# Two dense blocks handed to the gather, W2 in single steps, casts on ScalarE: one relational graph layer

## The chip, the cores and the metric

The kernel runs on one core of a Trainium2 chip. A core has TensorE (PE, matrix products; its weight loads, PEld, run beside them), VectorE (DVE), ScalarE (ACT), GpSimd (POOL) and SyncE (SP, which here only issues transfers). Sixteen DMA engines serve all queues. The metric is the device time of one execution in microseconds (us); the kernel before is given by the median of three runs, and one execution was profiled.

## The reference: what is computed

A graph of 3125 nodes with 128 features and 100000 edges, sorted by destination, each with one of 8 types, goes through four layers. The first three (three GCN steps, one sum over in-edges with a linear map, one GIN layer with batch norm) are not touched. The fourth is a relational layer applied twice, with 128 to 256 and 256 to 128 features:

```python
def rgcn_layer(x, src, dst, etype, W, W_root, b, num_rels):
    h = jnp.einsum('ni,rio->rno', x, W)
    msg = h[etype, src]
    seg = dst * num_rels + etype
    sums = jax.ops.segment_sum(msg, seg, num_segments=N * num_rels)
    cnt = jax.ops.segment_sum(jnp.ones(msg.shape[0], x.dtype), seg, num_segments=N * num_rels)
    mean = sums / jnp.maximum(cnt, 1.0)[:, None]
    agg = mean.reshape(N, num_rels, do).sum(axis=1)
    return agg + x @ W_root + b

h = jax.nn.relu(rgcn_layer(x, src, dst, edge_type, W1, root1, b1, 8))
h = rgcn_layer(h, src, dst, edge_type, W2, root2, b2, 8)
x = _layernorm(x + h)
```

For each node and each edge type it takes the mean over the in-edges of that type, maps it with that type's weights and adds the eight. The kernel must return the last x, 3125 x 128 in fp32.

## The kernel before

The nodes are cut into 25 blocks of 128 (the last one partly filled). Tile, the layer above the instruction set, puts in the semaphores and decides the order of each engine's instructions when the program is built: it goes by the order in which the program was written, and moves a later instruction ahead where by its own times an earlier one is not ready. On the chip each engine then follows its fixed order.

**Lists and masks.** `relations()`, a generator that is advanced while the GCN steps run, prepares what the relational layers need. It counts in-edges by type, gathers the edge lists of the blocks that will be "gathered" (`NG` of them, 34 lists of 128 edges a block, 15 for the last; lines 373 to 423), and then builds, for the `ND` = 14 "dense" blocks, a count matrix per type: how many edges run from node s to node d, as bytes in DRAM (`rel`, lines 425 to 466). Edges of the other 11 blocks stay as lists: `gsrc` holds the source row, `gkey` the place of destination and type within a window of 24 nodes. If a list doesn't fit its window, a flag makes the whole fallback `general` run.

**First relational layer, preparation (lines 831 to 838).** `split2` splits x into two fp32r parts, `xs`. `store3` splits it again into three bf16 parts and writes them to DRAM as the row table `xt_d` (7 chunks; a ScalarE copy, a DVE subtract, a ScalarE copy, a DVE subtract, a store on SP's queue; two buffers). No gather can start before the whole table is written.

**Dense blocks (lines 881 to 887, `relation` at 752).** The blocks go in chunks of four or three (`CH`; the first four chunks are the 14 dense blocks). For each chunk and each of 8 types, five groups: a byte mask is loaded, cast to fp32r (two of five groups on ScalarE, line 766, three on DVE, line 768, by the tuple `casts`), and multiplied by the two parts of x, ten products a group (line 771). Masks have six byte buffers and three cast ones. 4 x 8 x 5 = 160 groups; the product of a type is scaled into `z`.

**Gathered blocks (`gathered`, line 782), between the groups.** It is a generator: a step is one tile, in which POOL gathers 128 table rows (an indirect DMA into one of twelve `gx` buffers, line 805) and TensorE multiplies the three bf16 parts by a one-hot matrix that DVE made (lines 797 and 813), or the end of a block, `put1`. After each dense group, `relation` advances it by `rate` = 2.2 steps on average, beginning 14 steps late; what is left is done after the last dense group.

**A finished chunk (`linear1`, line 840).** When the eight types of a chunk are summed, dense or gathered, W1 and the root map are applied (16 fp32 products and two more, lines 851 and 853), then ReLU into `hT`; then, for each block, twice: two fp32 products with W2 for four types (line 861) and `store3` into the DRAM table `ht_d`. The profile records an fp32 product as two.

**Second relational layer.** It is built the same way on `ht_d`, type by type, with all casts on ScalarE (line 944), the same `CH`, the same 14 dense blocks and the rate 2.2. Its first gather waits for all of `ht_d`.

Of the kernel before, what the change touches and what calls it, by code (L numbers as in the profile page):

```python
# [21 lines left out]
P = 128  # L22
# [36 lines left out]
HL = 49 * 64  # L59
ND = 14  # L60
NG = NB - ND
GT = [34] * (NG - 1) + [15]
# [10 lines left out]
def listed(ctx: ExitStack, tc: tile.TileContext, p: dict, out: bass.AP, bad):  # L73
# [27 lines left out]
    adj_t = dram.tile([NB, P, NB, P], BF, name="adj_t")  # L101
    rel = [dram.tile([ND, P, NB, P], U8, name=f"rel{r}") for r in range(R)]
    inv_d = dram.tile([R * SB, 2 * P], F32, name="inv_d")
# [44 lines left out]
    with ExitStack() as lists, tc.tile_pool(name="f_ps", bufs=1, space=PSUM) as psum:  # L148
# [193 lines left out]
        def relations():  # L342
# [31 lines left out]
            for g in range(NG):  # L374
                b = ND + g
                nc.gpsimd.indirect_dma_start(
                    out=ge[:, g, :], out_offset=None, in_=pk[:],
                    in_offset=bass.IndirectOffsetOnAxis(ap=gi[:GM, b // 2, b % 2 : b % 2 + 1], axis=0),
                )
# [9 lines left out]
            for o, a in ((gd, gf[0]), (gt, gf[1])):  # L389
                t = psum.tile([P, 512], F32, name="mi", tag="mi", bufs=2)  # L390
                for g in range(NG):
# [7 lines left out]
            nc.vector.scalar_tensor_tensor(gsrc[1], gy, float(NP), gsrc[0], op0=OP.mult, op1=OP.add)  # L399
            gw = bg.tile([P, NG, GM], F32, name="gw")  # L400
            gb = bg.tile([P, NG, GM], F32, name="gb")
            nc.gpsimd.iota(gw, pattern=[[0, NG], [4, GM]], base=-8, channel_multiplier=0,
                           allow_small_or_imprecise_dtypes=True)
            nc.gpsimd.iota(gb, pattern=[[P, NG], [0, GM]], base=ND * P, channel_multiplier=0,
                           allow_small_or_imprecise_dtypes=True)
# [12 lines left out]
            nc.tensor.matmul(t[:, :1], ones, gs, start=True, stop=True)  # L418
            nc.vector.tensor_add(gs, t[:, :1], begin[:, ND // 2, ND % 2 : ND % 2 + 1])
            bad2 = bg.tile([P, 1], I32, name="bad2")  # L420
# [12 lines left out]

            units = [(b, u) for b in range(ND) for u in range(64 // PU)]
            nxt = hots(*units[0])
# [276 lines left out]
    x3 = xa  # L712
    DENSE = [c for c in CH if c[0] < ND]
    with tc.tile_pool(name="f_rel", bufs=1) as rp, tc.tile_pool(
# [22 lines left out]

        def store3(rows, x):

            n = x.shape[1]  # L740
            t = rp.tile([P, 4, 3, D], BF, name="t3", bufs=2)
            a, b, c = [t[:, :n, i, :] for i in range(3)]
            e = rp.tile([P, 4, D], F32, name="e3", bufs=2)[:, :n, :]
            nc.scalar.copy(a, x)  # L744
            nc.vector.tensor_sub(e, x, a)  # L745
            nc.scalar.copy(b, e)
            nc.vector.tensor_sub(c, e, b)
            nc.sync.dma_start(rows, t[:, :n].rearrange("p b i c -> p b (i c)"))

        ahead = [0.0]  # L750

        def relation(r, m0, nb, pieces, work, rate, casts):

            acc = psum.tile([P, 512], F32, name="acc", tag="acc", bufs=2)
            w = nb * P
            for g in range(5):
                m8 = rp.tile([P, 4, 5, P], U8, name="m8", bufs=6)
                nc.sync.dma_start(
                    m8[:, :nb].rearrange("p b k d -> p b (k d)"),
                    rel[r][m0 : m0 + nb, :, 5 * g : 5 * g + 5].rearrange("b p k d -> p b (k d)"),  # L760
                )
                m = rp.tile([P, 5, 4 * P + 8], F32R, name="m", bufs=3)
                v = m[:, :, :w].rearrange("p k (b d) -> p k b d", d=P)
                src = m8[:, :nb].rearrange("p b k d -> p k b d")
                if casts[g]:
                    nc.scalar.copy(v, src)  # L766
                else:
                    nc.vector.tensor_copy(v, src)  # L768
                for k in range(5):
                    for i, x in enumerate(pieces):  # L770
                        nc.tensor.matmul(  # L771
                            acc[:, :w], x[:, 5 * g + k, :],
                            m[:, k, :w],
                            start=(g == 0 and k == 0 and i == 0), stop=(g == 4 and k == 4 and i == 1),
                        )
                ahead[0] += rate
                while ahead[0] >= 1.0:
                    next(work, None)
                    ahead[0] -= 1.0
            return acc[:, :w]  # L780

        def gathered(table, rows, put):


            for g in range(NG):
                b = ND + g
                wn = min(P, HL - b * P)
# [35 lines left out]
        with tc.tile_pool(name="f_z", bufs=1) as zp:  # L823
# [8 lines left out]
            hT = rp.tile([P, 2, NP], F32, name="hT", tag="big", bufs=2)  # L832
            nc.vector.memset(hT[:, :, HL:], 0.0)
            for m0, nb in CH:
                split2(xs, m0, nb, x3[:, m0 : m0 + nb, :])
            for m0, nb in CH:
                store3(xt_d[m0 * P : (m0 + nb) * P].rearrange("(b p) c -> p b c", p=P),
                       x3[:, m0 : m0 + nb, :])

            def linear1(z, m0, nb):  # L840
# [6 lines left out]
                for a in range(2):  # L847
                    o = psum.tile([P, 512], F32, name="mi", tag="mi", bufs=2)
                    c = slice(a * P, (a + 1) * P)
                    for r in range(R):  # L850
                        nc.tensor.matmul(o[:, :w], w1[:, r, c], z[:, r, :w],  # L851
                                         start=(r == 0), stop=False)
                    nc.tensor.matmul(o[:, :w], root1[:, c], x3t[:, :w], start=False, stop=True)
                    nc.scalar.activation(hT[:, a, m0 * P : m0 * P + w], o[:, :w], AF.Relu,
                                         bias=b1[:, a : a + 1])

                for b in range(m0, m0 + nb):
                    for r in range(0, R, 4):
                        o = psum.tile([P, 512], F32, name="mi", tag="mi", bufs=2)
                        for a in range(2):  # L860
# [3 lines left out]
                        store3(ht_d.rearrange("(r n) c -> n r c", r=R)[b * P : (b + 1) * P, r : r + 4],  # L864
                               blocks(o))

            zg = [None]

            def put1(b, wn, acc, inv):
                m0, nb = [c for c in CH if c[0] <= b < c[0] + c[1]][0]  # L870
                if b == m0:
# [6 lines left out]

            work = gathered(xt_d, gsrc[0], put1)
            ahead[0] = -14  # L880
            for m0, nb in DENSE:
                z = zp.tile([P, R, 512], F32, name="z", bufs=2)
                for r in range(R):
                    inv = load_inv(r, m0, nb)
                    acc = relation(r, m0, nb, xs, work, 2.2, (0, 1, 0, 1, 0))
                    nc.vector.tensor_mul(z[:, r, : nb * P], acc, inv)
                linear1(z, m0, nb)
            for _ in work:
                pass

        with tc.tile_pool(name="f_hr", bufs=1) as hp:
# [44 lines left out]

            work = gathered(ht_d, gsrc[1], put2)
            ahead[0] = -14
            hr = fetch(0)
            for r in range(R):  # L940
                nxt = None
                for i, (m0, nb) in enumerate(DENSE):
                    inv = load_inv(r, m0, nb)
# [630 lines left out]
```

## Time and profile before

| | |
|---|---|
| median of 3 runs | 2251.15 us (2241.75 to 2253.26) |
| profiled execution | 2257.92 us, span 2256.1 us |
| mean granted TensorE clock | 0.921 of full |
| busy share: PE, PEld, DVE, ACT, POOL | 86, 62, 56, 47, 40% |
| first relational layer | 968.7 to 1697.3 us |
| second relational layer | 1697.3 to 2256.1 us |
| first gather of layer 1 starts | 1006.6 us |
| dense products, both layers | 3200 recorded, 780.2 us busy |

A line of a group names the source line, engine, operation, what it writes and reads, the shape and the count; then busy us and mean ns of one; then the engine's idle time before them and what ended it. A line of a timeline gives the start, the duration, the engine and the instruction, how many alike were merged, and in brackets the idle time before it and its releaser. TensorE's products overlap, so a product's duration is longer than the time until the next one starts; prices are taken from start to start. Some products are missing from the records.

### The profile page before, as it was taken

How to read it: one execution, taken by the hardware profiler on the slowest of the kernel's cores; microseconds unless marked ns; L12 is line 12 of the kernel's file. 1: busy time of each engine (PE TensorE's matmuls, PEld its weight loads, DVE VectorE, ACT ScalarE, POOL GpSimd, SP SyncE). 2: the span in 40 equal slices, each digit the busy share in tenths (PEclk: the TensorE clock that was granted, in tenths of full speed). 3: DMA queues.
4: the chain of work that ended last, by engine and by line, in shares of the span. 5: the costliest groups of instructions: out<-in, count | busy, mean ns of one | idle time of the engine just before them, and what ended most of it. 6: DMA issues, size and time to landing. Idle time of an engine off the chain costs nothing.

```text
span 2256.1 us, 31992 instructions
## 1 busy us (share of the span) xinstructions
PE 1932.3 (86%) x12201; PEld 1394.4 (62%) x12201; DVE 1271.3 (56%) x2303; ACT 1058.1 (47%) x1151; POOL 903.2 (40%) x898
## 2 busy tenths in 40 slices
PE   1667769999999699778998999999878899888984
PEld 1445536666665588555776667567536777767763
DVE  4888889999996563363443445344236434334423
ACT  1666644544442465541231333232227667666761
POOL 3222121121120000017747357437524766666664
PEclk9776679999999899888998999999989999999996
DMA  3444466788787788075655567456538877777762
GB/s 91 182 175 165 178 194 210 264 291 271 261 270 244 244 262 243 20 206 137 192 155 160 155 179 204 129 157 180 140 102 256 231 207 226 208 215 225 209 172 71
DMA packets 384636, 433.06 MB, mean 192 GB/s; under 512 B 28731, under 2 KB 350301, under 8 KB 384472
## 3 DMA queue, kind: packets, MB, share of 16 engines
q1 hardware_dynamic: 314318, 278.95, 40.3%
q0 software_dynamic: 45920, 119.66, 17.9%
q10 hardware_dynamic: 24234, 32.31, 5.0%
q8 instruction: 97, 1.59, 0.3%
q14 instruction: 67, 0.55, 0.1%
HBM read 319.22 MB, written 111.58 MB: 191 GB/s over the span
## 4 chain that ended last, share of the span: by engine, by line
PE 59%; DVE 17%; issue 7%; DMA 7%; ACT 4%; POOL 3%; another core or an unknown queue 2%; ACTq 0%; DVEq 0%; SPq 0%; POOLq 0%
PE acc L771 25%; PE ga L813 8%; PE acc L534 7%; PE acc L569 6%; PE mi L861 4%; PE mi L851 4%; DMA g<-dsf,irow 3%; DVE lo L161 2%; DVE rhq L161 2%; PE bld L448 2%; ACT m L766 2%; DVE hi L161 2%; DVE rlo L161 1%; POOL gx L805 1%
## 5 line engine op out<-in xcount | busy, mean ns | idle before, releaser
L771 PE MATMUL acc<-m,hilo 128*128 128x384 f32 (+1 forms) x3200 | 780.2, 387 | 50.5 <-issue 35.3
L771 PEld LDWEIGHTS acc<-m,hilo 128*128 128x128 f32 x3200 | 582.1, 195 | 139.6 <-issue 62.0
L766 ACT CAST m<-m 128x2560 fp32r<-128x2560 uint8 (+1 forms) x224 | 455.4, 2061 | 449.4 <-PE ga L813 121.9
L805 POOL DMA_INDIRECT gx<-xt_d,gsrc x355 | 391.3, 1102 | 566.0 <-DMA inv<-inv_d 306.5
L805 POOL DMA_INDIRECT gx<-ht_d,gsrc x355 | 362.5, 1021 | 220.5 <-issue 79.3
L534 PE MATMUL acc<-m,parts 128*128 128x512 bf16 (+1 forms) x1575 | 334.6, 359 | 11.6 <-DMA r_L_gnn_g<-in_L_gnn_g 10.5
L813 PE MATMUL ga<-oh,gx 128*128 128x192 bf16 (+1 forms) x2442 | 266.4, 246 | 63.4 <-issue 35.3
L813 PEld LDWEIGHTS <-gx 128*128 128x128 bf16 x2442 | 178.6, 100 | 157.2 <-issue 124.7
L797 DVE TENSOR_TENSOR oh<-iota,gkey 128x768 bf16<-128x768 bf16 (+1 forms) x188 | 100.1, 533 | 270.6 <-PE ga L813 128.0
L534 PEld LDWEIGHTS <-parts 128*128 128x128 bf16 x1575 | 152.9, 98 | 135.5 <-issue 13.9
L768 DVE CAST m<-m 128x2560 fp32r<-128x2560 uint8 (+1 forms) x96 | 152.0, 1584 | 115.6 <-issue 36.4
L455 ACT CAST rb<-bld 128x800 uint16<-128x800 f32 x179 | 143.7, 828 | 125.8 <-PE bld L448 120.7
L462 POOL DMA_DIRECT2D rel<-rb x112 | 64.4, 583 | 286.9 <-ACT rb L455 182.8
L569 PE MATMUL acc<-mf,halves 128*128 128x512 f32 (+1 forms) x700 | 154.2, 378 | 18.0 <-ACT mf L566 17.8
L569 PEld LDWEIGHTS acc<-mf,halves 128*128 128x128 f32 x700 | 128.0, 190 | 38.3 <-issue 18.7
L161 DVE TENSOR_TENSOR lo<-iota,kT 128x2048 bf16<-128x2048 bf16 x100 | 122.0, 1220 | 1.5 <-PE bld L271 1.5
L271 PE MATMUL bld<-hi,lo 128*128 128x50 bf16 x1600 | 75.8, 202 | 41.1 <-DVE hi L161 25.9
L566 ACT CAST mf<-m 128x2560 fp32r<-128x2560 bf16 (+1 forms) x42 | 88.2, 2102 | 48.1 <-PE acc L569 38.6
L448 PE MATMUL bld<-rhq,rlo 128*128 128x200 bf16 x896 | 107.7, 253 | 1.7 <-DVE rb L457 1.0
L745 DVE TENSOR_TENSOR e<-mi,t 128x512 f32<-128x512 f32 x50 | 34.3, 687 | 129.9 <-ACT t L744 125.7
L271 PEld LDWEIGHTS <-lo 128*128 128x128 bf16 x1600 | 64.9, 108 | 66.5 <-DVE hi L161 25.8
L448 PEld LDWEIGHTS <-rlo 128*128 128x128 bf16 x896 | 82.9, 98 | 36.5 <-issue 8.3
(216 smaller groups left out, 2137.2 us busy)
## 6 DMA issues: line engine op xcount, KB each, us to landing
m<-rel SPq DMA_DIRECT2D x160, 320.0 KB
rel<-rb POOLq DMA_DIRECT2D x112, 400.0 KB
m<-adj SPq DMA_DIRECT2D x60, 640.0 KB
m<-rel SPq DMA_DIRECT2D x160, 240.0 KB
m<-adj_t SPq DMA_DIRECT2D x40, 640.0 KB
m<-adj SPq DMA_DIRECT2D x45, 480.0 KB
adj_t<-at SPq DMA_DIRECT2D x25, 800.0 KB
adj<-av SPq DMA_DIRECT2D x25, 800.0 KB
```

What stands on the lines that cost most here:

```text
L161: nc.vector.tensor_tensor(o, (iota2 if of is None else of)[:, None, :width, :].to_broadcast([P, PU // 2, width, 2]), k[:, :, None, :].to_b ...
L271: nc.tensor.matmul(pt[:, j, : 2 * NB], lo[:, j // 2, :, j % 2], hi[:, j // 2, :, j % 2], start=True, stop=True)
L448: nc.tensor.matmul(pt[:, k, : R * NB], lo[:, j // 2, :, j % 2], hq[:, j // 2, :, j % 2], start=True, stop=True)
L455: nc.scalar.copy(o, src)
L534: nc.tensor.matmul(o, x[:, k, :], m(k - k0), start=(k == 0 and i == 0), stop=(k == NB - 1 and i == 2))
L569: nc.tensor.matmul(acc[:, :w], x[:, 5 * g + k, :], mf[:, k, :w], start=(g == 0 and k == 0 and i == 0), stop=(more is None and g == 4 and k ...
L766: nc.scalar.copy(v, src)
L768: nc.vector.tensor_copy(v, src)
L771: nc.tensor.matmul(acc[:, :w], x[:, 5 * g + k, :], m[:, k, :w], start=(g == 0 and k == 0 and i == 0), stop=(g == 4 and k == 4 and i == 1),)
L797: nc.vector.tensor_tensor(oh[:, : nt // 2], iota2[:, None, : GW * R, :].to_broadcast([P, nt // 2, GW * R, 2]), gkey[:, g, t : t + nt].rear ...
L805: nc.gpsimd.indirect_dma_start(out=gx.rearrange("p i c -> p (i c)"), out_offset=None, in_=table[:], in_offset=bass.IndirectOffsetOnAxis(ap ...
L813: nc.tensor.matmul(acc[:, a:z], gx[:, i, :], oh[:, t % 4 // 2, a - c0 : z - c0, t % 2], start=(a // 512 not in seen), stop=(t == GT[g] - 1 ...
```

## The change

`ND` = 14 is split in two. `ND1` = 12 is the number of dense blocks in the first relational layer, `ND2` = 14 that of the second and of the masks that are built. The first layer so has 13 gathered blocks, 423 tiles for 355, and the lists are prepared for 13. Its chunks are all four blocks long, and the last one (`CH1`): three dense chunks, 120 groups of 512 columns. The rate becomes 3.7.

The W2 part of `linear1` becomes a generator, `project`, put in the list `todo`. `one_step` advances it by half a block; it is called once in each dense group, between the products and the gather steps, once per remaining gather step after the dense groups, and until the list is empty.

In the first layer all casts go to ScalarE, but for those of the very first relation. The subtracts of the table's seven splits go from DVE to POOL (`eng`). Two scratch tiles of the list preparation share buffers with earlier ones.

```diff
-ND = 14
-NG = NB - ND
+ND1, ND2 = 12, 14
+NG = NB - ND1
+CH1 = ((0, 4), (4, 4), (8, 4), (12, 4), (16, 4), (20, 4), (24, 1))
...
-            gw = bg.tile([P, NG, GM], F32, name="gw")
-            gb = bg.tile([P, NG, GM], F32, name="gb")
+            gw = bg.tile([P, NG, GM], F32, name="gw", tag="ge")
+            gb = bg.tile([P, NG, GM], F32, name="gb", tag="it")
...
-        def store3(rows, x):
+        def store3(rows, x, eng=nc.vector):
...
-            nc.vector.tensor_sub(e, x, a)
+            eng.tensor_sub(e, x, a)
             nc.scalar.copy(b, e)
-            nc.vector.tensor_sub(c, e, b)
+            eng.tensor_sub(c, e, b)
...
+        todo = []
+
+        def one_step():
+            while todo and next(todo[0], None) is None:
+                todo.pop(0)
...
+                one_step()
                 ahead[0] += rate
                 while ahead[0] >= 1.0:
                     next(work, None)
...
-            for g in range(NG):
-                b = ND + g
+            for b in range(nd, NB):
+                g = b - ND1
...
                 store3(xt_d[m0 * P : (m0 + nb) * P].rearrange("(b p) c -> p b c", p=P),
-                       x3[:, m0 : m0 + nb, :])
+                       x3[:, m0 : m0 + nb, :], nc.gpsimd)
...
+                todo.append(project(m0, nb))
+
+            def project(m0, nb):
                 for b in range(m0, m0 + nb):
                     for r in range(0, R, 4):
...
                         store3(ht_d.rearrange("(r n) c -> n r c", r=R)[b * P : (b + 1) * P, r : r + 4],
                                blocks(o))
+                        yield True
...
-            for m0, nb in DENSE:
+            for m0, nb in CH1:
+                if m0 >= ND1:
+                    break
...
-                    acc = relation(r, m0, nb, xs, work, 2.2, (0, 1, 0, 1, 0))
+                    acc = relation(r, m0, nb, xs, work, 3.7,
+                                   (0, 1, 0, 1, 0) if m0 + r == 0 else (1, 1, 1, 1, 1))
                     nc.vector.tensor_mul(z[:, r, : nb * P], acc, inv)
                 linear1(z, m0, nb)
             for _ in work:
-                pass
+                one_step()
+            while todo:
+                one_step()
```

More of the change, by code (lines that the diff above doesn't have):

```diff
@@ L101, in listed @@
     adj_t = dram.tile([NB, P, NB, P], BF, name="adj_t")
-    rel = [dram.tile([ND, P, NB, P], U8, name=f"rel{r}") for r in range(R)]
+    rel = [dram.tile([ND2, P, NB, P], U8, name=f"rel{r}") for r in range(R)]
     inv_d = dram.tile([R * SB, 2 * P], F32, name="inv_d")
@@ L374, in relations @@
             for g in range(NG):
-                b = ND + g
+                b = ND1 + g
                 nc.gpsimd.indirect_dma_start(
@@ L399, in relations @@
             nc.vector.scalar_tensor_tensor(gsrc[1], gy, float(NP), gsrc[0], op0=OP.mult, op1=OP.add)
-            gw = bg.tile([P, NG, GM], F32, name="gw")
-            gb = bg.tile([P, NG, GM], F32, name="gb")
+            gw = bg.tile([P, NG, GM], F32, name="gw", tag="ge")
+            gb = bg.tile([P, NG, GM], F32, name="gb", tag="it")
             nc.gpsimd.iota(gw, pattern=[[0, NG], [4, GM]], base=-8, channel_multiplier=0,
                            allow_small_or_imprecise_dtypes=True)
-            nc.gpsimd.iota(gb, pattern=[[P, NG], [0, GM]], base=ND * P, channel_multiplier=0,
+            nc.gpsimd.iota(gb, pattern=[[P, NG], [0, GM]], base=ND1 * P, channel_multiplier=0,
                            allow_small_or_imprecise_dtypes=True)
@@ L418, in relations @@
             nc.tensor.matmul(t[:, :1], ones, gs, start=True, stop=True)
-            nc.vector.tensor_add(gs, t[:, :1], begin[:, ND // 2, ND % 2 : ND % 2 + 1])
+            nc.vector.tensor_add(gs, t[:, :1], begin[:, ND1 // 2, ND1 % 2 : ND1 % 2 + 1])
             bad2 = bg.tile([P, 1], I32, name="bad2")
@@ L432, in hots @@
                 return lo, hq
-            units = [(b, u) for b in range(ND) for u in range(64 // PU)]
+            units = [(b, u) for b in range(ND2) for u in range(64 // PU)]
             nxt = hots(*units[0])
@@ L712, in listed @@
     x3 = xa
-    DENSE = [c for c in CH if c[0] < ND]
     with tc.tile_pool(name="f_rel", bufs=1) as rp, tc.tile_pool(
@@ L780, in relation, with gathered @@
             return acc[:, :w]
-        def gathered(table, rows, put):
-            for g in range(NG):
-                b = ND + g
+        def gathered(table, rows, nd, put):
+            for b in range(nd, NB):
+                g = b - ND1
                 wn = min(P, HL - b * P)
@@ L835, in listed @@
                 split2(xs, m0, nb, x3[:, m0 : m0 + nb, :])
-            for m0, nb in CH:
                 store3(xt_d[m0 * P : (m0 + nb) * P].rearrange("(b p) c -> p b c", p=P),
-                       x3[:, m0 : m0 + nb, :])
+                       x3[:, m0 : m0 + nb, :], nc.gpsimd)
             def linear1(z, m0, nb):
@@ L865, in linear1 @@
                                blocks(o))
+                        yield True
             zg = [None]
             def put1(b, wn, acc, inv):
-                m0, nb = [c for c in CH if c[0] <= b < c[0] + c[1]][0]
+                m0, nb = [c for c in CH1 if c[0] <= b < c[0] + c[1]][0]
                 if b == m0:
@@ L877, in put1 @@
                     linear1(zg[0], m0, nb)
-            work = gathered(xt_d, gsrc[0], put1)
+            work = gathered(xt_d, gsrc[0], ND1, put1)
             ahead[0] = -14
-            for m0, nb in DENSE:
+            for m0, nb in CH1:
+                if m0 >= ND1:
+                    break
                 z = zp.tile([P, R, 512], F32, name="z", bufs=2)
@@ L935, in put2 @@
                         finish(m0, nb)
-            work = gathered(ht_d, gsrc[1], put2)
+            work = gathered(ht_d, gsrc[1], ND2, put2)
             ahead[0] = -14
@@ L941, in listed @@
                 nxt = None
-                for i, (m0, nb) in enumerate(DENSE):
+                for i, (m0, nb) in enumerate(c for c in CH if c[0] < ND2):
                     inv = load_inv(r, m0, nb)
```

## The prediction

> **What bounds the kernel now.** I read the busy share by stretches first, then the groups, then the timelines of TensorE, POOL and DVE in the first relational layer, where all but a few lines of the change lie. That layer runs from 968.7 to 1697.3 us. By stretch: until the first dense chunk is done, the second, the third, the fourth, and the rest (the columns are the stretch, its length, then busy us and instructions of TensorE, its weight loads, DVE, ScalarE and POOL, granted clock, DMA share, GB/s).
>
> ```profile
> 968.70:1120.20 151.50, 127.01 (x648) 94.94 (x647) 75.93 (x90) 50.56 (x41) 84.87 (x78) 0.88 0.68 189
> 1120.20:1298.50 178.30, 166.35 (x851) 118.45 (x849) 71.74 (x88) 51.47 (x54) 95.67 (x88) 0.95 0.55 158
> 1298.50:1474.00 175.50, 170.95 (x851) 120.18 (x850) 81.37 (x85) 55.42 (x49) 104.84 (x92) 0.99 0.62 173
> 1474.00:1616.50 142.50, 129.22 (x739) 99.49 (x739) 57.48 (x69) 38.13 (x34) 86.03 (x78) 0.95 0.59 165
> 1616.50:1697.30 80.80, 65.81 (x222) 32.27 (x219) 23.52 (x36) 22.17 (x32) 19.91 (x21) 0.89 0.33 100
> ```
>
> TensorE carries the layer, ScalarE is idle two thirds of it. But a POOL that issues without a pause is busy only three quarters by these figures. Its own timeline around 1336 us, and DVE's at that moment:
>
> ```profile
> 1334.83 0.95 POOL L805 DMA_INDIRECT gx<-xt_d,gsrc  x1 [0.30 <-issue]
> 1336.08 1.92 POOL L805 DMA_INDIRECT gx<-xt_d,gsrc  x1 [0.30 <-PE ga L813]
> 1338.30 0.95 POOL L805 DMA_INDIRECT gx<-xt_d,gsrc  x1 [0.30 <-issue]
> ```
>
> ```profile
> 1335.96 1.75 DVE L768 CAST m<-m 128x2560 fp32r<-128x2560 uint8 x1
> ```
>
> A gather left alone takes 0.95 + 0.30 = 1.25 us; one that meets a DVE cast lasts until the cast has ended. The groups give the mean, and that of layer 2, whose casts are all ScalarE's:
>
> ```profile
> L805 POOL DMA_INDIRECT gx<-xt_d,gsrc x355 | 391.3, 1102 | 566.0 <-DMA inv<-inv_d 306.5
> L805 POOL DMA_INDIRECT gx<-ht_d,gsrc x355 | 362.5, 1021 | 220.5 <-issue 79.3
> ```
>
> With the 0.30 us: 1.40 and 1.32 us a tile. The unit prices of TensorE come from its timeline: in a dense stretch, at a finished chunk, and at the layer's end.
>
> ```profile
> 1062.35 0.69 PE L813 MATMUL ga<-oh,gx 128*128 128x192 bf16 x6
> 1062.82 2.56 PE L771 MATMUL acc<-m,hilo 128*128 128x512 f32 x10
> 1065.22 0.69 PE L813 MATMUL ga<-oh,gx 128*128 128x192 bf16 x6
> ...
> 1120.25 0.60 PE L845 MATMUL mi<-ident,xa 128*128 128x128 f32 x4
> 1120.69 7.03 PE L851 MATMUL mi<-z,w 128*128 128x512 f32 x16
> ...
> 1136.14 7.43 PE L861 MATMUL mi<-wr,hT 128*128 128x512 f32 x16
> 1143.00 2.33 PE L771 MATMUL acc<-m,hilo 128*128 128x384 f32 x10
> ...
> 1679.12 7.37 PE L861 MATMUL mi<-wr,hT 128*128 128x512 f32 x16
> 1687.92 3.96 PE L861 MATMUL mi<-wr,hT 128*128 128x512 f32 x8 [1.43 <-DVE e L745]
> ```
>
> From start to start: a dense group of 512 columns 2.40 us; a gathered tile (three products) about 0.24; linear1 of four blocks, 1120.25 to 1136.14, 15.9; a W2 step (half a block, recorded as four products) 6.86/4 = 1.72, and 2.27 in the tail, where 8 steps fill 1679.1 to 1697.3. A dense group of 384 columns takes 1.84 (1177.29 to 1179.12, the same view).
>
> **What the Trainium skill says.** "SBUF — State Buffer", section "Who interferes with whom": a cast on VectorE in a two-port mode shuts GpSimd out of its port, so descriptors are not written; a tensor_tensor takes only the read side. The trace agrees (1.92 against 0.95 us), and near the one-hot compares of 0.55 us the gather mostly stays at 0.95. "TensorE: Matmul & The Clock Gate", section "HAM oscillation — how this bites in real kernels": waits between products drop TensorE to half clock. The trace agrees: a 384-column group takes 3.35 us at 1209.57 after a starved stretch. "GPSIMD Engine Reference", section "3.1 Elementwise — side-by-side cycle accounting": a two-input fp32 add of 2048 takes 4497 ns there; for 512, about 1.2 us is an estimate from it. No POOL subtract is in this trace; DVE's takes 0.69.
>
> **The change, part by part.** *Dense to gathered.* 80 groups of 2.40 and 80 of 1.84 become 120 of 2.40: 339 to 288 us, -51. Tiles go from 355 to 423: +68 x 0.24 = +16. Chunks of four, not three: linear1 from 98 (3 x 15.9, 3 x 12.1, one of about 14) to 102 (6 x 15.9 and one of about 7), +4. The 50 W2 steps stay, 86. TensorE's demand falls from 608 to 577, -31, in a layer of 729. *The rate.* POOL gets 3.7 steps a group, 13 of 436 being block ends, so 3.6 tiles: 4.5 us at 1.25, where TensorE needs 2.40 + 0.86 = 3.26. POOL's demand rises from 355 x 1.40 = 497 to 423 x 1.25 = 529. So POOL sets the pace of every dense group without other work; twelve gx buffers let it run 15 us ahead.
>
> *ScalarE casts.* 2.33 us a group, plus a W2 step's two copies (0.58 + 0.62): 3.5, under 4.5. Behind POOL's pace this costs nothing; at TensorE's 3.26 with a step in each group it would add 0.3 a group. What it buys is the 1.25. *W2 in steps.* A step makes a group 4.98 us, about POOL's 4.5: 16 groups in 40 are so filled. Queued on SP between mask loads are the same 50 stores. Before, steps already alternated with dense groups after the first four of a chunk, so the gain lies with POOL, which sat blocked behind linear1 and the first four steps:
>
> ```profile
> 1147.62 0.94 POOL L805 DMA_INDIRECT gx<-xt_d,gsrc  x1 [18.47 <-PE ga L813]
> ```
>
> *Row table.* The seven splits have two subtracts each, now 1.2 instead of 0.69: +1 us a table chunk, in pairs (two buffers), so +4 before the first gather (1006.6 us); no DVE cast stands ahead of them any more (gain up to 3), but ScalarE's casts of 2.33 do stand ahead of its copies (loss up to 8). I take +4. *List preparation.* 13 lists for 11: two more index gathers and DVE work a fifth wider on some 15 instructions, where DVE is 378.5 of 400 us busy (300 to 700): +2.
>
> The layer then, in stretches. (1) Groups 0 to 39: 134 steps, 131 tiles. 1006.6 + 4 + 131 x 1.25 + 4 (landing) = 1178; TensorE alone would be done at 1105. It ended at 1120 before: 58 late, with 59 more tiles done. (2) To group 80: two linear1 31.8, 16 groups with a step 80, 24 at POOL's pace 24 x 4.5 - 15 = 93, joints (block-end multiply of 1.98 on DVE and what follows) 8: 213, so 1391. (3) To group 117, where blocks 20 to 23 end: 31.8 + 80 + 21.3 x 4.5 - 15 + 8 = 201: 1592. (4) linear1 15.9, 2.7 groups 13.5, linear1 17.9, six tiles with six steps 12, the last block 10, nine steps of 2.27 20: 89, so 1681. Against 1697.3 that is -16; with +2 for the lists, -14. What waits on the layer's end, layer 2, is untouched (559 us), and its mask loads are still issued ahead.
>
> The profiled run took 2257.92, its span 2256.1; -14 gives 2242 for the span and about 2244 for that run. The runs shown have a median of 2251.15, 7 below, so about 2238. A change of 0.5%, 11 us, is about what a measurement of this kernel tells from none.
>
> **Bounds.** Each 0.01 us a tile costs 2.9 us, since about 290 tiles (131 + 24 x 3.6 + 21 x 3.6) are on the path: 1.25 is the floor, 1.32 (layer 2's mean) gives +20; I take the floor because layer 2's mean holds the work of its fetches, which this layer lacks. Cold clock in starved groups: 0 to +25, I take none, as 72% busy stretches (3.26 of 4.5) mostly stayed warm around 1580. Stutters: in five or so stretches of about 10 us (1198 to 1208 is one) TensorE went at one product in 0.4 to 0.7 us with no releaser named; slack behind POOL may hide them now, 0 to -25; I take none. POOL's subtracts: -3 to +10.
>
> **The rivals.** *Slower: the gather's rate.* If tiles come at 1.36 us, stretches 1 to 3 lose 32 us: about 2270. It decides from 1.30 on, and measures as slower from 1.34. For it: 1.32 in layer 2, 1.40 now. Against it: the 0.95s in unbroken rows wherever DVE doesn't cast. *Far faster: overlap holds.* If dense groups may pass the gather while it is late, only POOL's floor counts: 1010.6 + 529 + 4 + a tail of 60 = 1604, -93; half of that is about 2205. For it: before, twelve groups ran ahead of the first gather. Against it: after it, the order is strict, one dense product per tile, then 2.2 tiles a group. *No change: a trade.* The 58 us lost in stretch 1 may be won back exactly; steps were interleaved anyway: 2251. *Not as said.* If blocks 12 or 13 broke the list's windows, the whole fallback would run after; in these inputs they hold 4015 and 4182 edges (limit 4352) and every tile lies within its 24 nodes.
>
> **How the numbers follow.** Forecast, 0 to -40 around -14: 0.52, of which 0.33 measures as faster and 0.19 as no change. Slower rival, +11 and more: 0.34. Far faster, beyond -40: 0.11. Exact trade, slightly above zero: 0.03. Fallback: below 0.01, left out. So 0.44 faster, 0.22 same, 0.34 slower. The range reaches from the far rival's milder half, 2195, to 2280, the gather at 1.39 us; the forecast's own is 2211 to 2251. Cases of both signs are in it because TensorE's saving and POOL's load are nearly equal.
>
> **What would show it.** First dense chunk done near 1178, second near 1391; gathers at 1.25 us without a DVE cast beside them and POOL unbroken through stretch 1; TensorE waiting for gx there; W2 products in pairs among dense groups. Wrong if gathers stay at 1.3 and more, if TensorE is at half clock in stretch 1, if ScalarE rather than POOL ends TensorE's waits, or if the first gather starts after 1020.

## The result

| | before | changed | ratio (95% interval) |
|---|---|---|---|
| time | 2249.84 us | 2320.72 us | 1.0322 (1.0293 to 1.0351) |
| profiled execution's span | 2256.1 us | 2311.1 us | |
| first relational layer ends | 1697.3 us | 1757.4 us | |
| layer 2, from there to the end | 558.8 us | 553.7 us | |

The change made the kernel 3.2% slower. The forecast, 2238 us with a range of 2195 to 2280, is missed by 83 us. All of the loss shows by the end of the first relational layer; layer 2 is 5 us shorter. By stretch of the changed kernel (the same columns as in the prediction; the cuts are the three moments at which a dense chunk's linear1 starts, the third being that of blocks 20 to 23, then the layer's end and the program's end):

```profile
974.20:1195.30 221.10, 163.60 (x857) 117.33 (x858) 31.08 (x46) 91.57 (x48) 142.75 (x146) 0.86 0.53 150
1195.30:1439.90 244.60, 210.58 (x1040) 141.99 (x1038) 56.04 (x85) 116.49 (x81) 145.87 (x149) 0.92 0.56 158
1439.90:1667.60 227.70, 202.54 (x990) 136.59 (x990) 52.08 (x80) 107.52 (x76) 131.45 (x133) 0.93 0.56 158
1667.60:1757.40 89.80, 80.71 (x248) 39.68 (x248) 25.92 (x40) 28.83 (x45) 5.76 (x7) 0.96 0.31 94
1757.40:2311.10 553.70, 477.99 (x2875) 383.43 (x2874) 223.86 (x401) 349.01 (x214) 364.01 (x355) 0.93 0.71 204
```

The chunks end at 1195, 1440 and 1668, forecast 1178, 1391 and 1592; the last stretch is as long as forecast, 90 us. So each of the three stretches in which dense groups and gathers share TensorE lost 17 to 32 us against the forecast. The groups show that neither the gather nor POOL's new subtracts did more than a small part of it:

```profile
L812 POOL DMA_INDIRECT gx<-xt_d,gsrc x423 | 415.6, 982 | 278.2 <-PE ga L820 127.4
...
L746 POOL TENSOR_TENSOR e<-xa,t 128x512 f32<-128x512 f32 (+1 forms) x7 | 8.6, 1238 | 278.3 <-DVE mv L126 266.0
```

A gather takes 0.98 + 0.30 = 1.28 us for the 1.25 of the forecast, by its own price of 2.9 us for each 0.01 some 9 us of the layer, and where POOL waits, it is mostly for TensorE to free a buffer. TensorE's own waits in this layer (what waited, for what, us in total, times, the longest) are the surprise:

```profile
PE ga L820 <- issue: 68.6, 89, 2.7
PE acc L777 <- issue: 17.5, 31, 2.3
PE ga L820 <- DMA gx<-xt_d,gsrc: 16.5, 20, 4.2
PE mi L858 <- DVE z L885: 12.0, 2, 11.2
```

Its idle time before gathered products is mostly "issue": nothing that the profile names ended it. A forecast with POOL as the pacemaker asks for the third line there. One such place, in the timeline of all engines ("remote" is a release whose sender the profile does not name):

```profile
1378.84 2.16 PEld L777 LDWEIGHTS acc<-m,hilo 128*128 128x128 f32 x10
1378.86 2.56 PE L777 MATMUL acc<-m,hilo 128*128 128x512 f32 x10
...
1382.12 0.10 PEld L820 LDWEIGHTS <-gx 128*128 128x128 bf16 x1 [0.40 <-issue]
1382.54 0.95 POOL L812 DMA_INDIRECT gx<-xt_d,gsrc  x1 [0.30 <-issue]
1382.82 0.33 PE L820 MATMUL ga<-oh,gx 128*128 128x192 bf16 x2 [0.87 <-issue]
...
1384.22 0.19 PEld L777 LDWEIGHTS acc<-m,hilo 128*128 128x128 f32 x1 [0.51 <-issue]
1384.92 2.78 PE L777 MATMUL acc<-m,hilo 128*128 128x512 f32 x5 [0.90 <-issue]
...
1385.65 0.69 DVE L900 TENSOR_TENSOR z<-acc,inv 128x512 f32<-128x512 f32 x1 [9.87 <-remote]
1385.69 2.34 ACT L772 CAST m<-m 128x2560 fp32r<-128x2560 uint8 x1 [8.37 <-remote]
1385.93 0.94 POOL L812 DMA_INDIRECT gx<-xt_d,gsrc  x1 [2.44 <-remote]
```

The dense group at 1378.86 looks done by 1381.4. But VectorE's multiply of that very group, ScalarE's cast into a buffer of an older one, and POOL's gather are all released only at 1385.6 to 1385.9, at once. In between TensorE starts one instruction in 0.7 us. The Trainium skill, "Perfetto Trace Analysis", section "Tensor Engine Instruction (MATMUL, LD_WEIGHTS)", says that the end of a product is estimated and its start observed; the late releases agree that the shown end need not be when others learn of it. The trace's record of TensorE's signals (its semaphore updates) shows the same: none between 1378.60 and 1385.62, then five within 0.3 us. So for some 4 us TensorE had everyone waiting for it. Whether it stood still, or worked and only its signals were held back, these lines do not tell. The products that follow run at half the granted clock (0.51 from 1385.6 to 1388.4). I call this a slow stretch. Such places were in the trace of before too ("stutters" in the prediction; its example of half clock at 1209.57 stands right behind the one of 1198 to 1208).

To count them I matched the n-th gather with its products, in program order, and took every place where three or more successive starts of TensorE's products lie 0.55 us and more apart. Where at the end of such a place at least three tiles, gathered over 2 us earlier, were still unused, rows were in hand; otherwise TensorE was simply waiting for rows. (A gather's packets, 98,368 bytes in the queue's order, are through 2.06 us after POOL's instruction at the median.) In the layer, before has 9 slow stretches with rows in hand, 66 us in all; the changed kernel 21, 135 us. The counts are rough. A second count (starts within 0.12 us taken as one, pieces less than 6 us apart joined) gives 11 of 79 us and 20 of 158 us; for the kernels below too it moves single numbers by as much, and leaves the large differences as they are.

### The profile page after: what moved, and what is told of

Read it like the earlier page. It is cut to its first block, busy times and chain, and to the rows that moved or that the text cites. A ratio compares the mean times of both kernels' runs of the same rounds, so it can differ in the third digit from the quotient of the medians.

```text
span 2311.1 us, 31728 instructions
## 1 busy us (share of the span) xinstructions
PE 1920.9 (83%) x12039; PEld 1356.1 (59%) x12039; DVE 1138.5 (49%) x2208; ACT 1193.1 (52%) x1204; POOL 947.2 (41%) x982
## 4 chain that ended last, share of the span: by engine, by line
PE 59%; DVE 15%; issue 10%; DMA 7%; ACT 4%; POOL 3%; another core or an unknown queue 2%; ACTq 0%; DVEq 0%; POOLq 0%; SPq 0%
PE acc L777 23%; PE ga L820 9%; PE acc L536 8%; PE acc L571 6%; PE mi L858 4%; PE mi L871 3%; DMA g<-dsf,irow 2%; PE bld L450 2%; DVE lo L163 2%; DVE rhq L163 2%; POOL gx L812 2%; DVE hi L163 1%; DMA gx<-xt_d,gsrc 1%; DVE rlo L163 1%
## 5 line engine op out<-in xcount | busy, mean ns | idle before, releaser
L772 ACT CAST m<-m 128x2560 fp32r<-128x2560 uint8 (+1 forms) x277 | 593.3, 2173 | 421.6 <-remote 136.2
L777 PE MATMUL acc<-m,hilo 128*128 128x512 f32 (+1 forms) x2800 | 735.5, 406 | 57.1 <-issue 43.9
L777 PEld LDWEIGHTS acc<-m,hilo 128*128 128x128 f32 x2800 | 526.4, 199 | 164.6 <-issue 71.9
L812 POOL DMA_INDIRECT gx<-xt_d,gsrc x423 | 415.6, 982 | 278.2 <-PE ga L820 127.4
L804 DVE TENSOR_TENSOR oh<-iota,gkey 128x768 bf16<-128x768 bf16 (+1 forms) x206 | 109.9, 534 | 630.4 <-PE ga L820 358.4
L820 PE MATMUL ga<-oh,gx 128*128 128x192 bf16 (+5 forms) x2676 | 295.1, 248 | 107.0 <-issue 77.3
L820 PEld LDWEIGHTS <-gx 128*128 128x128 bf16 x2676 | 201.5, 100 | 217.1 <-issue 170.4
L571 PEld LDWEIGHTS acc<-mf,halves 128*128 128x128 f32 x700 | 128.0, 190 | 37.4 <-issue 18.5
L746 POOL TENSOR_TENSOR e<-xa,t 128x512 f32<-128x512 f32 (+1 forms) x7 | 8.6, 1238 | 278.3 <-DVE mv L126 266.0
L858 PE MATMUL mi<-z,w 128*128 128x512 f32 (+1 forms) x224 | 92.2, 567 | 14.8 <-DVE z L885 12.0
```

The costliest lines, as they stand in the source:

```text
L571: nc.tensor.matmul(acc[:, :w], x[:, 5 * g + k, :], mf[:, k, :w], start=(g == 0 and k == 0 and i == 0), stop=(more is None and g == 4 and k ...
L777: nc.tensor.matmul(acc[:, :w], x[:, 5 * g + k, :], m[:, k, :w], start=(g == 0 and k == 0 and i == 0), stop=(g == 4 and k == 4 and i == 1),)
L804: nc.vector.tensor_tensor(oh[:, : nt // 2], iota2[:, None, : GW * R, :].to_broadcast([P, nt // 2, GW * R, 2]), gkey[:, g, t : t + nt].rear ...
L812: nc.gpsimd.indirect_dma_start(out=gx.rearrange("p i c -> p (i c)"), out_offset=None, in_=table[:], in_offset=bass.IndirectOffsetOnAxis(ap ...
L820: nc.tensor.matmul(acc[:, a:z], gx[:, i, :], oh[:, t % 4 // 2, a - c0 : z - c0, t % 2], start=(a // 512 not in seen), stop=(t == GT[g] - 1 ...
L858: nc.tensor.matmul(o[:, :w], w1[:, r, c], z[:, r, :w], start=(r == 0), stop=False)
```

## The experiments

Each job ran on one chip, and the chips are not alike: before takes 2151 to 2156 us on three of them and 2242 to 2262 us on four, the first one included. Ratios are taken against before on the same chip. I call the two kinds the 2150 chips and the 2250 chips.

### Which part costs

The move undone, the other edits kept (`e1_nd14`):

```diff
-ND1, ND2 = 12, 14
+ND1, ND2 = 14, 14
 NG = NB - ND1
-CH1 = ((0, 4), (4, 4), (8, 4), (12, 4), (16, 4), (20, 4), (24, 1))
+CH1 = CH
...
-                    acc = relation(r, m0, nb, xs, work, 3.7,
+                    acc = relation(r, m0, nb, xs, work, 2.2,
```

> The changed kernel with the move of blocks 12 and 13 undone (14 dense blocks, chunks of four and three, rate 2.2); steps of W2, ScalarE casts and the row table stay. Theory A (TensorE slows down when too many short gathered products stand between two dense groups, and the move did that): the loss goes, 2195 to 2245 us. Rival B (the gather's pace of 1.28 us a tile is paid, as forecast): 355 tiles for 423 save at most 68 x 1.28 = 87, TensorE's 31 come back: 2240 to 2275. Rival D (single W2 steps or ScalarE casts cost the time): still 2290 or more.

The move alone, the other edits undone (`e2_move_alone`):

```diff
             for m0, nb in CH:
                 split2(xs, m0, nb, x3[:, m0 : m0 + nb, :])
+            for m0, nb in CH:
...
-                       x3[:, m0 : m0 + nb, :], nc.gpsimd)
+                       x3[:, m0 : m0 + nb, :])
...
-                todo.append(project(m0, nb))
+                for _ in project(m0, nb):
+                    pass
...
-                                   (0, 1, 0, 1, 0) if m0 + r == 0 else (1, 1, 1, 1, 1))
+                                   (0, 1, 0, 1, 0))
```

> The changed kernel with everything but the move undone: W2 in bulk, two of five casts on ScalarE, row table on VectorE after all of the splits; 12 dense blocks and rate 3.7 stay. Theory A: the move costs the time and the other edits save some: 2325 to 2380 us. Rival B: gathers meet VectorE's casts, 1.40 us a tile: 2330 to 2370, and gathers are longer than 0.95 us. Rival D: 2240 to 2280.

On a 2150 chip the first took 2110.7 us, 0.9809 (0.9774 to 0.9843) of before, the second 2246.2, 1.0445 (1.0411 to 1.0480). The loss belongs to the move; the other three edits together gain. Rival D is out. As ratios of a before of 2250 us, the first lies in A's range (0.976 to 0.998) and below B's (0.996 to 1.011), the second in both. Before itself is faster here, so the ranges need not carry over, and A and B stay unseparated.

### Gathers or short products

On the same chip, TensorE relieved (`e3_one_part`) and POOL relieved (`e4_half_gather`):

```diff
-                    for i in range(3):
+                    for i in range(3 if table is ht_d else 1):
...
```

> The changed kernel, but in the first layer TensorE multiplies only the first of the three bf16 parts of a gathered tile (two parts are left out of the result): one product and one weight load a tile for three, about 0.16 us x 423 = 68 us of TensorE, all gathers as before. Theory A (TensorE's short products set the pace of the groups, and its slow stretches come from them): slow stretches with one instruction in 0.4 to 0.7 us vanish, 2215 to 2255. Rival B (POOL's pace): TensorE waits for rows instead, no less than 2300.

```diff
-                    gx = rp.tile([P, 3, D], BF, name="gx", bufs=12)
-                    nc.gpsimd.indirect_dma_start(
+                    if t % 2 == 0 or table is ht_d:
+                        gx = rp.tile([P, 3, D], BF, name="gx", bufs=12)
+                        nc.gpsimd.indirect_dma_start(
...
```

> The changed kernel, but in the first layer POOL gathers only every second tile; the other tiles multiply the rows of the tile before (half the rows are left out of the result). TensorE's products are all there. Theory A: 2300 to 2325, the slow stretches stay. Rival B (POOL's pace of 1.28 us a tile): POOL's 543 us fall to 271, the layer falls to TensorE's 577 and more, 2230 to 2270.

1.0056 (1.0039 to 1.0072) and 0.9700 (0.9667 to 0.9734). As ratios, both lie outside the ranges of both theories. Relieving POOL is worth far more than relieving TensorE, so POOL's pace is paid here. The trace with half the gathers has no slow stretch with rows in hand; but the changed kernel turned out to have none either on such a chip (`g1_after`, below), so theory A is not tested by it. And these were ratios on a chip where the changed kernel itself had not been timed, so I ran it again.

### The changed kernel again, and its gain without the move

Beside the changed kernel itself (`f1_after_again`): 20 gather buffers (`f2_gx20`), and two variants of the version with 14 dense blocks, one with the old casts (`f3_nd14_dve_casts`), one with W2 in bulk (`f4_nd14_bulk`).

```diff
-                    gx = rp.tile([P, 3, D], BF, name="gx", bufs=12)
+                    gx = rp.tile([P, 3, D], BF, name="gx", bufs=20)
```

> The changed kernel itself once more, beside the three below, so that all stand on one chip. Before took 2250 us where the change was first measured and 2151 where the first four runs were made, so the ratio is what counts. Theory P (every gathered tile costs POOL 1.28 us and TensorE waits for it, wherever it is run): 1.025 to 1.04 of before. Theory S (the loss was TensorE's slow stretches of the first chip, one instruction in 0.7 us with the rows already there, which the runs of the other chip show seldom): 0.99 to 1.015 there.

> The changed kernel with 20 gather buffers in both relational layers instead of 12. Theory P: POOL can get 20 tiles, 25 us, ahead instead of 15 while TensorE is in linear1 and in groups with W2 steps, so that each of the two later chunks starts its starved groups 8 tiles better off: 15 to 30 us less than the changed kernel. Theory S: within 5 us of the changed kernel.

> The changed kernel with 14 dense blocks and the old rate as in the first experiment (0.981 of before there), and two of five casts on ScalarE again, three on VectorE: W2 in steps and POOL's table stay. If the gathers undisturbed by casts made the gain (355 x 0.13 us = 46): 0.99 to 1.005 of before. If W2 in steps made it: 0.975 to 0.985.

> The changed kernel with 14 dense blocks and the old rate, and W2 in bulk behind linear1 as before: ScalarE's casts and POOL's table stay. If W2 in steps made the gain: 0.99 to 1.005 of before. If the undisturbed gathers made it: 0.975 to 0.985.

The job fell on a 2250 chip. The changed kernel: 1.0297 (1.0256 to 1.0339), with 26 slow stretches, 172 us. Twenty buffers made it worse, 1.0396 (1.0367 to 1.0424), with 29 of 184 us, which neither theory expected. On this chip, where TensorE waits for rows only 9.9 us, room to run ahead is no help; on a 2150 chip it was not tried. With 14 blocks and the old casts 0.9873 (0.9832 to 0.9913); with W2 in bulk 1.0015 (1.0002 to 1.0029). So the gain of the other edits hangs on the W2 steps; the gathers freed from VectorE's casts (969 ns a gather with ScalarE's casts, 1070 with the old ones) brought nothing that shows.

### On a 2150 chip

The changed kernel (`g1_after`), the two relieved kernels again (`g2_half_gather`, `g3_one_part`), and one with few mask loads (`g4_few_masks`):

```diff
-                m8 = rp.tile([P, 4, 5, P], U8, name="m8", bufs=6)
-                nc.sync.dma_start(
+                if g == 0 or rate < 3:
+                    m8 = rp.tile([P, 4, 5, P], U8, name="m8", bufs=6)
+                    nc.sync.dma_start(
...
```

> The changed kernel, as the base of the three below on their chip. Where before takes about 2250 us: 1.03 of before, with some 25 slow stretches of TensorE in the first relational layer. Where before takes about 2150: theory S (slow stretches are what the forecast missed) 0.985 to 1.01; theory P (POOL's pace alone makes the change slower) 1.02 to 1.04.

> POOL gathers only every second tile of the first layer, the products of TensorE all stay (half of the rows are left out of the result). It gave 0.970 of before where before takes 2151 us. If slow stretches come from TensorE's many short instructions, they stay or increase here (3.3 us a group, the same products), and the time is 50 us or less under the changed kernel. If they come with TensorE running dry behind POOL, they vanish with the waits, and the time is 110 us or more under the changed kernel, on either chip.

> Two of three products and weight loads of each gathered tile of the first layer are left out (two bf16 parts miss in the result), all gathers stay. If short instructions of TensorE bring the slow stretches, they go: 90 us or more under the changed kernel where it has them. If they come with running dry behind POOL, they stay: TensorE saves at most its 68 us, of which POOL's pace hides a part: 30 to 65 us under the changed kernel.

> In the first relational layer the mask bytes of a relation are loaded for the first of its five groups only and cast five times (the counts of the other four are left out of the result): 96 of 120 loads of 320 KB less. If traffic into the memory that TensorE reads from makes its slow stretches, they get rarer and the time falls by 30 us or more where it has them. If not: within 10 us of the changed kernel.

The changed kernel took 2179.06 us, 1.0146 (1.0116 to 1.0175): slower here too, by half as much. It lies between the ranges of theory P and theory S. Its stretches, cut at the same events:

```profile
974.00:1175.60 201.60, 151.11 (x858) 105.96 (x859) 40.13 (x59) 101.40 (x58) 142.78 (x146) 0.93 0.61 174
1175.60:1389.30 213.70, 196.06 (x1040) 133.99 (x1038) 56.09 (x83) 114.73 (x79) 139.27 (x145) 1.00 0.62 177
1389.30:1591.60 202.30, 188.84 (x991) 128.82 (x990) 52.73 (x80) 109.36 (x77) 131.30 (x137) 0.99 0.61 180
1591.60:1682.10 90.50, 81.82 (x248) 40.49 (x248) 26.20 (x40) 28.76 (x45) 9.91 (x11) 0.94 0.31 97
1682.10:2174.70 492.60, 454.21 (x2874) 372.51 (x2874) 223.53 (x401) 351.80 (x214) 355.21 (x355) 0.96 0.78 230
```

1175.6, 1389.3, 1591.6 and 1682.1: the forecast's 1178, 1391, 1592 and 1681, each within 3 us. TensorE's waits in this layer, the largest two:

```profile
PE ga L820 <- DMA gx<-xt_d,gsrc: 69.7, 92, 3.6
PE acc L777 <- issue: 12.3, 1, 12.3
```

Here TensorE waits for rows, by name; the one "issue" is the layer's start. There is no slow stretch with rows in hand, and the kernel is slower all the same. Half the gathers: 0.9717 (0.9688 to 0.9747), 91 us less than the changed kernel, between the two forecasts of 50 or less and 110 or more; one part of three: 1.0061 (1.0034 to 1.0089), 18.5 us less, under both forecasts, though 68 us of products are gone by the price, since TensorE then waits 96.1 us for rows instead of 69.7. Few masks: 1.0133 (1.0104 to 1.0162), no difference, but on a chip without slow stretches this can't clear the mask traffic of them.

### What brings the slow stretches, and where before gains

On a 2250 chip, before itself for its trace (`h1_before`), and half the gathers (`h2_half_gather`):

> The kernel before itself, for its trace on this chip. Where it takes about 2150 us, the changed kernel's first relational layer was read at 974 to 1682.5 us, within 3 us of each of the forecast's marks (1178, 1391, 1592, 1681). If the forecast failed by taking slow stretches in the trace of before for part of the kernel: no slow stretch of TensorE with rows in hand, the layer ends at 1640 to 1660 instead of 1697, and the three chunk ends come 10 to 15 us apart earlier than 1120, 1298 and 1474. If the forecast mis-sized a step: the layer ends at 1685 or later, and the difference lies in layer 2. Where it takes about 2250: the same trace as first seen, ends at 1690 to 1705.

> POOL gathers only every second tile of the first layer, TensorE's products all stay (half of the rows are left out of the result). Where before takes 2150: 0.971 again. Where it takes 2250 (changed kernel at 1.030): if the slow stretches come from TensorE's many short instructions, they stay, 0.99 or more; if they come with running dry behind POOL, they vanish from the first layer, 0.95 to 0.965.

Before took 2267.43 us, its layer ended at 1702.5, with 13 slow stretches. Half the gathers: 0.9574 (0.9540 to 0.9609). TensorE's instructions in the layer are all there and closer together, and yet only one slow stretch is left, right after the wait for the first rows. So many short instructions alone don't bring them. Of the causes that I had named, that leaves the gathers' traffic, or that TensorE runs dry. `i1_filler` keeps all gathers and adds work:

```diff
+        done = [0]
...
+                done[0] += 1
+                if rate > 3 and done[0] > 10 and not todo:
+                    fill = psum.tile([P, 512], F32, name="mi", tag="mi", bufs=2)
+                    for k in range(7):
+                        nc.tensor.matmul(fill[:, :w], pieces[0][:, 5 * g + k % 5, :], m[:, k % 5, :w],
+                                         start=(k == 0), stop=(k == 6))
                 one_step()
```

> The changed kernel with work added: in each group of 512 columns of the first layer that has no W2 step, from the eleventh on, TensorE makes seven more dense products into a tile that nobody reads, 7 x 0.24 = 1.7 us, some 65 groups, 110 us of TensorE in all. All gathers stay. TensorE then needs about 5.0 us a group, a little over POOL's 4.5, and does not run dry. If running dry brings the slow stretches: they go from the filled groups; where before takes 2250, 0.995 to 1.03 of before, no slower than the changed kernel for all the added work; where it takes 2150, 1.02 to 1.035. If the gathers' traffic beside dense groups brings them: they stay, 1.06 to 1.08 where before takes 2250.

It ran on a 2250 chip beside `i2_nd14` (the kernel of the first experiment) and `i3_before`:

> The changed kernel with 14 dense blocks and the old rate, the first experiment again: it gave 0.981 of before where before takes 2151 us. Where it takes 2250: 0.96 to 0.98, since TensorE runs dry less than before and its slow stretches should get fewer.

> The kernel before for its trace. Where it takes about 2150: its first relational layer ends at 1640 to 1660 us, with hardly a slow stretch of TensorE, so that the forecast's layer end of 1681 is slower than it. If it ends at 1685 or later, the gain lies elsewhere.

The group of the filler's added products, and TensorE's timeline in a part that had slow stretches before (the lines of this kernel stand one and seven further down):

```profile
L787 PE MATMUL mi<-m,hilo 128*128 128x512 f32 x518 | 136.9, 400 | 3.7 <-issue 3.6
```

```profile
1385.35 2.57 PE L778 MATMUL acc<-m,hilo 128*128 128x512 f32 x10
1387.75 1.79 PE L787 MATMUL mi<-m,hilo 128*128 128x512 f32 x7
1389.39 1.20 PE L827 MATMUL ga<-oh,gx 128*128 128x192 bf16 x12
1390.37 2.56 PE L778 MATMUL acc<-m,hilo 128*128 128x512 f32 x10
```

Groups follow one another at 5.0 us without a pause. 518 products are 518 x 0.24 = 124 us of added work; the time is 1.0357 (1.0321 to 1.0393) of before, where the changed kernel had 1.0322 and 1.0297 on two other chips of that kind: about 10 us for 124. The changed kernel was not timed on this chip itself, so the 10 us are good to a few us only. It is a little above what I expected, and far from the 1.06 to 1.08 of the rival. 9 slow stretches with rows in hand are left, 56 us, for 21 and 26. The gathers are all there, but 3.6 of them now come in 5.0 us instead of 4.5, so that their traffic is a tenth thinner. With 14 blocks 0.9930 (0.9908 to 0.9952): less than expected, since 8 slow stretches, 46 us, are left. Before took 2245.35, layer end 1687.4.

The last run, `j1_before`, fell on a 2150 chip.

> The kernel before for its trace, once more. Where it takes about 2150: its first relational layer ends at 1640 to 1660 us (worked out: 2150 less the 492 us of layer 2 that the changed kernel shows there), with hardly a slow stretch of TensorE while rows are in hand. If it ends at 1685 or later, the forecast's sum has another error that the changed kernel's marks hide.

Before took 2157.53 us there. Its stretches (the layer's start, the chunk ends, the layer's end, the program's end), and TensorE's largest wait in the layer:

```profile
968.70:1113.40 144.70, 125.17 (x650) 95.70 (x651) 75.56 (x88) 50.07 (x41) 84.92 (x78) 0.90 0.72 198
1113.40:1277.50 164.10, 158.02 (x849) 114.89 (x848) 72.35 (x89) 51.68 (x54) 94.81 (x88) 0.99 0.61 172
1277.50:1446.60 169.10, 167.47 (x848) 119.13 (x847) 79.81 (x84) 55.35 (x48) 106.90 (x94) 1.00 0.64 179
1446.60:1581.90 135.30, 122.77 (x743) 95.83 (x742) 58.55 (x71) 41.33 (x36) 83.77 (x74) 1.00 0.61 172
1581.90:1658.80 76.90, 64.24 (x218) 32.31 (x216) 22.50 (x34) 18.89 (x31) 23.13 (x24) 0.89 0.37 108
1658.80:2155.70 496.90, 453.22 (x2875) 372.27 (x2874) 223.89 (x401) 352.81 (x215) 359.88 (x355) 0.96 0.80 228
```

```profile
PE ga L813 <- DMA gx<-xt_d,gsrc: 37.4, 39, 3.7
```

The layer of before ends at 1658.8 here, not at 1697.3, and that is not scatter: in its three traces from 2250 chips it ended at 1697.3, 1702.5 and 1687.4. (The stretch counted here is the start of a linear1, 1624.8 to 1629.4: products of W1 at a granted clock of 0.51 after a wait for rows, so no slow stretch of the kind above. The same place stands at 1663.5 in the first trace of before.) All of it side by side (the first relational layer; slow stretches with rows in hand, counted as above):

| kernel | before takes there | layer ends | slow stretches | wait for rows |
|---|---|---|---|---|
| before | 2250 | 1697.3 | 9, 66 us | 15.0 us |
| before (`j1_before`) | 2156 | 1658.8 | 1, 4 us | 37.4 us |
| changed | 2250 | 1757.4 | 21, 135 us | 16.5 us |
| changed (`f1_after_again`) | 2262 | 1778.2 | 26, 172 us | 9.9 us |
| changed (`g1_after`) | 2151 | 1682.1 | none | 69.7 us |
| half the gathers (`h2_half_gather`) | 2261 | 1601.1 | 1, 18 us | 6.3 us |
| half the gathers (`g2_half_gather`) | 2151 | 1591.1 | none | 6.9 us |
| filler (`i1_filler`) | 2242 | 1771.2 | 9, 56 us | 8.5 us |
| 14 blocks (`i2_nd14`) | 2242 | 1662.6 | 8, 46 us | 10.9 us |
| 14 blocks (`e1_nd14`) | 2151 | 1614.5 | none | 10.4 us |

## Why the prediction was wrong

The step that failed is the comparison of 1681 with 1697.3 ("Against 1697.3 that is -16"), with the term behind it, the stutters ("0 to -25; I take none"). Its mark for the changed kernel was built from undisturbed prices: 2.40 us a group, 1.72 a W2 step, 1.25 a tile. It was then set against a trace of before that contained the slow stretches. The two sides were not of one kind. The term for the slow stretches also had the wrong sign: the change made them more, not fewer.

- Without slow stretches the sum should have read 1681 - 1658.8 = +22 us, and one trace of each on two 2150 chips gives 1682.1 - 1658.8 = +23, with 1.0146 in the time. TensorE's busy time in the layer falls from 637.7 to 617.8 us (the sums of the stretches; 31 were forecast), but its idle time grows by 38, of which 32 are its wait for rows (37.4 to 69.7). The demand saved was real; it was given back behind POOL. That POOL sets the pace was right, and the marks within 3 us are not luck in the main (in the first, a gather that starts 3 us early makes up for 131 tiles at 0.02 us more); what was missing is that before, without slow stretches, ends its layer sooner still.
- With them, before ends 1697.3 - 1658.8 = 38.5 us later and the changed kernel 1757.4 - 1682.1 = 75.3 us later. I had said that slack behind POOL may hide them. The halved gathers and the filler point to the reverse: where TensorE has slack, they multiply. 23 - 38.5 + 75.3 = 60 us is what the layer lost. This splits the loss by chip and not by cause: the 38.5 and 75.3 us hold all that differs between the two kinds of chip, the lower clock too.

Point by point.

- *Gather at 1.25 us without VectorE's casts*: nearly right (982 ns + 0.30, and 966 + 0.30 on the 2150 chip), and the slower rival with its 1.34 us falls although the kernel did get slower.
- *Stretches 1 to 3 at POOL's pace, steps filling 16 of 40 groups*: right where nothing else disturbs.
- *ScalarE's casts cost nothing*: right; TensorE waited for casts less than 1 us in all.
- *The row table, +4*: no cost shows. From the first split of x to the first gather it is 37.5 us in both kernels on the first chip, 36.8 and 37.3 on the two 2150 chips. A subtract takes 1.24 us as estimated; but I overlooked, in the description too, that the diff puts each chunk's table part right behind its split, in one loop, which may have made up for it. No run separates the two.
- *List preparation, +2*: not to be told. The first dense product stands at 968.3 to 977.1 us in four traces of before and at 974.2 to 982.3 in three of the changed kernel.
- *Layer 2 untouched*: 553.7 for 558.8, and 492.6 for 496.9 on 2150 chips.
- *Overlap holds, -46* and *an exact trade*: neither.
- *Cold clock, 0 to +25, none taken*: 0.86 to 0.93 in the three stretches on the first chip, 0.93 to 1.00 where there are no slow stretches; so most of it goes with the same term.

A version that beats both kernels came out of it: 14 dense blocks with the other edits kept, 0.981 of before on a 2150 chip and 0.993 on a 2250 chip (0.987 on another one with the old casts), the W2 steps being what gains.

## What to carry to other kernels

A forecast made from undisturbed unit prices must be set against a before made from the same prices: rebuild the time of before first, and carry what the rebuild leaves over into both sides. Taking work from the busiest engine gains nothing where the engine that feeds it then sets the pace; spend the slack on work that is needed anyway (the W2 steps between groups), or leave the work where it was. And time the same pair on more than one chip before reading a difference of 2% as a property of the code: here one pair gave 1.015 and 1.032.

## What the runs showed of the hardware

Two things I had not expected. The same program takes 2151 to 2157 us on some chips and 2242 to 2267 on others, and about 40 of these 100 us lie in this layer, where TensorE has its slow stretches: one instruction in about 0.7 us for 2 to 18 us, rows landed, the other engines waiting for it; some 60 more lie in layer 2 (496.9 for 558.8 us in before). Second, on the chips that have them they go along with slack of TensorE: halving the gathers or adding idle products left fewer of them, more buffers did not.

What holds TensorE in them is open. Instruction supply comes to mind. The Trainium skill, "Runtime: NRT & Kernel Launch", section "Instruction fetch mechanics", says that blocks of 256 instructions are fetched while others run, mostly hidden; the trace has 96 packets of 16 KB in that queue. In the changed kernel they start at 1326.5, 1360.5, 1390.6 and 1417.4 us, the slow stretches at 1329.9, 1348.2, 1364.7, 1381.7, 1396.1 and 1409.7: by turns some 4 and some 21 us behind a packet, which looks like step. But the next four, at 1560.2, 1581.2, 1608.0 and 1625.4, lie 16.2, 12.6, 7.4 and 24.8 us behind one. And a late fetch would hold back starts, while in the place shown the signal of a group whose products had all started by 1381.1 came at 1385.6. Both speak against it and settle nothing.

The traces hold a mark that tells the two kinds of chip apart more sharply than the time. Of the signals that TensorE's instructions of this layer should give, those of the 2150 chips record nearly all (before 594 of 600, changed 614 of 622: `j1_before`, `g1_after`), those of the 2250 chips clearly fewer (485 of 600 and 562 of 622 in the first traces of the two). In layer 2 it is 517 and 516 of 520 against 448 and 453; ahead of the two layers all four record 99% and more. Before lacks more of them than the changed kernel, so this is no count of slow stretches. Whether the signals are merged, late or only not recorded, and whether the recording of the instructions has itself a part in the slow stretches, no run tests.

Whether they belong to the chip or to the hour in which a job ran on it can't be told from these runs either, since no two of the later jobs fell on one chip. And slack is only what they go along with: in the changed kernel 2 to 7 tiles were gathered and unused when each of the slow stretches between groups began, so none begins in a wait for rows itself.
